# A graph-convolution kernel: every third kept group of the last-but-one pass is sent in pairs, and the sums' rows are asked for earlier

## The chip, the cores and the metric

The kernel runs on one core of a Trainium2 chip. Its time is the device time of one launch in microseconds (us); of several runs the median is taken. Five engines work side by side, each through its own instructions in order, and wait for each other by semaphores: PE (TensorE, matrix products), DVE (VectorE), ACT (ScalarE), POOL (GpSimd, which here issues indirect DMAs) and SP (SyncE, which here issues plain DMAs).

## The reference

It is one message-passing layer on 12,500 nodes and 400,000 edges. The edges are sorted by `dst`, while `src` is random. `h` is gathered by `dst`, and the messages are summed by `src`.

```python
h = relu(layernorm(x))                              # [12500, 128]
h = h @ W_in2f.T
W = smu(edge_attr_20 @ W_f1.T + b_f1) @ W_f2.T + b_f2   # [400000, 128]
msg = h[dst] * W * edge_weight[:, None]
agg = segment_sum(msg, src, 12500)
out = x + smu(agg @ W_o1.T + b_o1) @ W_o2.T + b_o2
# smu(x) = ((1 + a) * x + (1 - a) * x * erf(mu * (1 - a) * x)) / 2,  a = 0.01, mu = 2.5
```

## The kernel before

**Units.** 128 edges are a tile, 4 tiles a group, 2 groups (8 tiles) a super. There are 391 supers (782 groups; the last has one tile). The supers are cut into ten passes of 56, 56, 56, 56, 46, 36, 36, 26, 16 and 7 supers (`PARTS`). The nodes are cut into 98 bins of 128.

**Sending.** A message is a row of 129 floats: 128 values and the place of its node inside its bin, plus a mark of the pass. It is written by an indirect DMA on POOL (`scatter_rows`, L1005; called a scatter from here on) into a buffer in DRAM, to row bin x capacity + slot. One scatter sends one tile, so 128 rows. The slot is a running count: `bins` adds up on DVE how often each bin has come (`so`), `count` turns that into a rank with triangular matrices on PE, `read` and `number` make the row index `ix` on DVE.

**Summing.** When a whole pass has been sent, its rows are read back while the next pass is sent. `begin` and `fetch` (L1036, SP) read the rows of several bins at once into one of four `rw` buffers (774 KB for passes whose sums take 12 rows per partition). `choose` (L1050, DVE) makes the 0/1 matrix `se` of which row belongs to which node. `add` (L1063, PE) multiplies the two per bin into a PSUM bank `pg` of four bins, and DVE adds the bank to `agg` (L1076). A new `fetch` is asked for when a buffer has been used up. `chores` says in which group of a pass these things begin: `times` returns the group at which the rows are asked for, the one at which the first `se` is made, and the one at which the products begin. From there the products are spread evenly over the rest of the pass (`lo`, `hi`, `parts`). The products of pass 7 are 98 bins x 3, those of pass 8 are 98 bins x 2; the trace shows each product as two records. From pass 7's sums on, each finished bank of the older sum is also multiplied by `w_o1` (`fold`, L1089, and a copy on ACT, L1090).

**Paired groups.** In passes 1 to 7 every 4th group (`EVERY`) is paired. Rows of its tiles 0 and 1 are matched with rows of tiles 2 and 3 that go to the same bin, so that two rows stand side by side and one scatter sends 128 pairs. `spread_keys` and `match` find the partners (PE, DVE), `rank_left` and `place_left` number the rows that are left, `permute` (L794, PE) brings the rows into order, and `take_pairs` (L805, L806, ACT) copies them out of PSUM. The rows that are left over make one more tile, `lt`, which is sent with a later group of the same pass (its "host"), where it is also counted. A paired group so takes 3 scatters and not 4.

**Kept groups.** The last two passes (8 and 9, `SENT_LAST`) are computed early: after every ninth super of passes 1 to 4 stands one super of these. Their messages, already multiplied by `w_o1`, are stored as `kept_rows` in DRAM, and their indices stay in `ix_kept`. When all other groups have been sent, the **closing loop** goes through these 46 groups. For each one, `refill` (L1665, SP) reads back the rows of the group four ahead into one of six `ms` buffers, `chores` sets up the sums of the pass before, `scatter` sends the group's four tiles, and `parts` does its share of the products. Before the loop stands a chain of small operations that forms a flag (L1668 to L1685). Behind the loop the last stage sums pass 9 and applies the output layer (L1716 to L1760).

**What sets the order.** Every engine but POOL goes through its instructions in the order in which the code is written; so does each queue. SP's reads for the sums and SP's refills stand in one queue, one behind the other.

```python
        for g in range(g1, NG):
            refill(g + 4)
            k = chores(g)
            scatter(g, back.pop(g))
            parts(hi)
            if g - g1 >= 2:
                old(g - g1 - 2)
            biased(g - g1 - 10)
```

## Time and profile before

| | |
|---|---|
| three runs | 5584.23, 5608.95 and 5618.83 us; median 5608.95 us |
| the profiled execution | 5585.07 us, of which the span from the first to the last instruction is 5583.3 us |
| mean granted TensorE clock | 0.82 of full speed |
| busy in the span | PE 69%, DVE 59%, POOL 53%, ACT 50% |
| scatters | 2668 and 138 before the closing loop, 181 in it |
| closing loop | first scatter at 5207.23 us, last one at 5509.91 us, end of the program at 5583.3 us |

Times in the rows are us from the start of the span, the length of one operation in a group is in ns. "busy, mean | idle before <-releaser" says how long a group of instructions was busy, how long one took, and how long the engine had stood idle just before them, with what ended most of it. Releaser "issue" means that the engine waited for nothing that the profile shows, "remote" that the releaser isn't among the recorded instructions. In the view by stretches, (x) is the number of records that begin or run in a stretch, PEclk the granted TensorE clock, and DMA share the busy part of the 16 DMA engines.

### The profile page before, as it was taken

How to read it: one execution, taken by the hardware profiler on the slowest of the kernel's cores; microseconds unless marked ns; L12 is line 12 of the kernel's file. 1: busy time of each engine (PE TensorE's matmuls, PEld its weight loads, DVE VectorE, ACT ScalarE, POOL GpSimd, SP SyncE). 2: the span in 40 equal slices, each digit the busy share in tenths (PEclk: the TensorE clock that was granted, in tenths of full speed). 3: DMA queues.
4: the chain of work that ended last, by engine and by line, in shares of the span. 5: the costliest groups of instructions: out<-in, count | busy, mean ns of one | idle time of the engine just before them, and what ended most of it. 6: DMA issues, size and time to landing. Idle time of an engine off the chain costs nothing. (4 is left out here: it accounts for less than half of the span.)

```text
span 5583.3 us, 86344 instructions
## 1 busy us (share of the span) xinstructions
PE 3853.0 (69%) x26034; PEld 3229.5 (58%) x26034; DVE 3306.8 (59%) x8547; ACT 2787.6 (50%) x7401; POOL 2934.9 (53%) x3031
## 2 busy tenths in 40 slices
PE   7566667667776776666776677777777667676557
PEld 3245446556665665555665566666666556566446
DVE  7766555556556666555666566656665556565336
ACT  6544455555555555555555555555454545544101
POOL 5556554544545555555545455455455555554564
PEclk9767778888888888888888788888888888888778
DMA  5756655556655555554555455555555545554567
GB/s 145 200 172 186 189 161 168 175 169 182 176 158 150 156 149 162 150 154 144 154 155 159 146 160 160 154 164 154 161 157 156 151 137 154 148 158 143 175 207 204
DMA packets 660449, 907.51 MB, mean 163 GB/s; under 512 B 181219, under 2 KB 446823, under 8 KB 659849
## 3 DMA queue, kind: packets, MB, share of 16 engines
q1 hardware_dynamic: 552553, 673.46, 42.5%
q0 software_dynamic: 100112, 216.17, 11.8%
q10 hardware_dynamic: 7312, 12.29, 0.6%
q8 instruction: 211, 3.46, 0.3%
q14 instruction: 261, 2.14, 0.1%
HBM read 507.13 MB, written 394.46 MB: 161 GB/s over the span
## 5 line engine op out<-in xcount | busy, mean ns | idle before, releaser
L1005 POOL DMA_INDIRECT buf<-ms,ix x2668 | 2587.5, 970 | 1898.6 <-issue 939.5
L880 ACT ACTIVATE hg<-ph,w_sb 128x128 f32<-128x128 f32 x2784 | 794.1, 367 | 1987.8 <-remote 1078.9
L1063 PE MATMUL pg<-se,rw 128*128 128x128 f32 x8232 | 1405.3, 313 | 507.6 <-DVE agg L1076 258.1
L1063 PEld LDWEIGHTS pg<-se,rw 128*128 128x128 f32 x8232 | 1248.3, 221 | 665.9 <-issue 296.2
L905 PE MATMUL pw<-w_f,ge 128*128 128x128 f32 x5568 | 1216.5, 345 | 443.2 <-DVE ms L935 382.9
L905 PEld LDWEIGHTS pw<-w_f,ge 128*128 128x128 f32 x5568 | 1022.4, 229 | 551.9 <-issue 326.5
L652 DVE SCALAR_TENSOR_TENSOR so<-irow_ps,hi_f,so 128x98 f16<-128x98 f32 x2846 | 902.6, 317 | 85.3 <-PE pg L825 3.9
L716 DVE TENSOR_REDUCE sl<-pc 128x4 f32<-128x392 f32 (+1 forms) x782 | 451.7, 578 | 591.5 <-remote 311.8
L935 DVE TENSOR_TENSOR ms<-pw,hg 128x512 f32<-128x512 f32 x558 | 383.1, 687 | 671.2 <-issue 414.9
L1050 DVE TENSOR_TENSOR se<-irow_ps,rw 128x1536 f32<-128x1536 f32 (+1 forms) x353 | 601.8, 1705 | 177.4 <-remote 114.6
L906 PE MATMUL pw<-wls,f 128*128 128x128 bf16 x2784 | 679.7, 244 | 2.6 <-issue 2.6
L601 ACT ACTIVATE oh<-oh,onesb 128x512 bf16<-128x512 bf16 x746 | 538.1, 721 | 24.2
L600 ACT ACTIVATE oh<-rbc,nrow 128x512 bf16<-128x512 uint8 x728 | 542.4, 745 | 0.0
L1005 POOL DMA_INDIRECT buf<-lt,ix x138 | 132.2, 958 | 578.6 <-DVE ix L739 566.3
L861 PE MATMUL ph<-hw,oh 126*128 126x128 bf16 x2784 | 311.4, 241 | 167.0 <-issue 106.7
L861 PEld LDWEIGHTS <-oh 126*128 126x128 bf16 x2784 | 244.3, 110 | 209.9 <-issue 188.2
L1076 DVE TENSOR_TENSOR agg<-agg,pg 128x512 f32<-128x512 f32 (+1 forms) x200 | 134.4, 673 | 384.1 <-remote 277.0
L906 PEld LDWEIGHTS <-f 128*128 128x128 bf16 x2784 | 316.9, 114 | 1.8 <-issue 1.8
L833 ACT ACTIVATE ge<-pu 128x512 f32<-128x512 f32 x448 | 273.2, 610 | 42.9 <-PE pu L825 13.4
L683 PE MATMUL pc<-so,tri 128*128 128x392 f16 (+1 forms) x644 | 234.7, 364 | 29.2 <-issue 19.6
L794 PE MATMUL pt<-cd,mt 128*128 128x129 f32 (+1 forms) x1656 | 233.0, 295 | 23.9 <-DVE at L774 22.3
L1005 POOL DMA_INDIRECT buf<-ms,ix_kept x181 | 174.5, 964 | 133.8 <-DMA ms<-kept_rows 81.6
(317 smaller groups left out, 4450.0 us busy)
## 6 DMA issues: line engine op xcount, KB each, us to landing
rw<-buf SPq DMA_DIRECT2D x300, 774.0 KB
f<-f_parts SPq DMA_DIRECT2D x370, 240.0 KB
buf<-zero SPq DMA_DIRECT2D x146, 387.0 KB
rbc<-rel_dram SPq DMA_DIRECT2D x389, 128.0 KB
buf<-ms,ix POOLq DMA_INDIRECT x2668
f_parts<-hs SPq DMA_DIRECT2D x106, 360.0 KB
rw<-buf SPq DMA_DIRECT2D x49, 645.0 KB
f_parts<-hs SPq DMA_DIRECT2D x108, 240.0 KB
```

The lines of the kernel that those rows point to most:

```text
L600: nc.scalar.activation(oh, loaded[s][1][:, o:o + n], AF.Abs, bias=pneg if s < FEW // SUP else nrow)
L601: nc.scalar.activation(oh, oh, AF.Relu, scale=-1.0, bias=onesb[:, 0:1])
L652: nc.vector.scalar_tensor_tensor(so[:, j], irow_ps[:, :NB], hi_f[:, t + j:t + j + 1], since, op0=ALU.is_equal, op1=ALU.add)
L716: nc.vector.tensor_reduce(sl[:, :n], pc[:, :n], op=ALU.max, axis=AX.X)
L861: nc.tensor.matmul(ph[:, j * P:(j + 1) * P], oh[:3 * WIN, a:a + P], hw[:3 * WIN, g % PER, :], start=True, stop=True)
L880: nc.scalar.activation(hg[:, j * P:(j + 1) * P], rows_of[g][:, j * P:(j + 1) * P], AF.Copy, scale=w_sb[:, t + j:t + j + 1])
L905: nc.tensor.matmul(pw[:, a:a + P], ge[:, a:a + P], w_f2, start=True, stop=False)
L906: nc.tensor.matmul(pw[:, a:a + P], fb[:, o + a:o + a + P], wls, start=False, stop=True)
L935: nc.vector.tensor_tensor(ms[:, :n, 0:P], pw.rearrange("p (j f) -> p j f", f=P)[:, :n], hg.rearrange("p (j f) -> p j f", f=P)[:, :n], op=A ...
L1005: i = nc.gpsimd.indirect_dma_start(out=(wide if g in host or g in paired else bufs)[k][:, :], out_offset=bass.IndirectOffsetOnAxis(ap=ix, ...
L1050: nc.vector.tensor_tensor(se[:, a:a + n], own.unsqueeze(1).to_broadcast([P, n, P]), rows_in[c][:, a:a + n, P:P + 1].to_broadcast([P, n, P] ...
L1063: nc.tensor.matmul(pgs[0][:, g, :], rows_in[c][:, o, 0:P], sel[c][:, o, :], start=(q == 0), stop=(q == Q[k] - 1))
```

## The change

- One super moves from pass 8 to pass 0 (`PARTS`: 57 and 15 for 56 and 16). The closing loop so has 44 groups instead of 46, and the loop before it two more that scatter.
- In pass 8 every third group (`LATE_EVERY`), eight in all, is paired. The matching is done in the closing loop when the group is sent: its keys are kept from before (`late_keys`), `spread_keys` and `match` stand two groups ahead of it, `permute` and `take_pairs` one group ahead. `refill` reads such a group in two halves, `ms` and `cd`.
- The rows that are left over aren't counted with a host. They are counted behind all others of the pass: `count_left` goes on from the pass's last count (`so_end`), `place_of_left` makes the index, and the scatter stands three groups behind the pair's own.
- `times`: the rows of pass 7 are asked for at group 1 of pass 8 instead of 2, and the products begin at group 2 instead of 4; for pass 8 and the groups of pass 9 it is 0 instead of 1, and 0 instead of 4.
- In the closing loop `chores` stands ahead of `refill`, and `parts` is cut in two halves.
- The flag is formed at the last group of pass 8, not before the loop. The old inputs that the last stage needs are kept in other places, since `mt` is in use. A row of ones (`ones1`) gives way to a row of another constant.

The diff, cut to what moves work (`g in paired` became `g in pair_no` in the functions that are left out):

```diff
-PARTS = (56, 56, 56, 56, 46, 36, 36, 26, 16, 7)
+PARTS = (57, 56, 56, 56, 46, 36, 36, 26, 15, 7)
 EVERY = 4
+LATE_EVERY = 3
...
+        LATE_END = eps_of[-1][0] * PER - 1
+        late_pairs = list(range(EARLY * PER + LATE_EVERY - 1, LATE_END - 3, LATE_EVERY))
+        pair_no = {g: i for i, g in enumerate(list(paired) + late_pairs)}
...
-            if g in paired:
+            if g in pair_no:
                 last[k] = so[:, GRP]
                 nc.vector.scalar_tensor_tensor(so[:, GRP], so[:, 1], 2.0, before, op0=ALU.mult, op1=ALU.add)
+            if g == LATE_END:
+                nc.vector.tensor_copy(so_end, last[k])
...
-            if g in paired:
-                key = cnt.tile([P, GRP], F32, name="key")
+            if g in pair_no:
+                key = cnt.tile([P, GRP], F32, name="key") if g in paired else late_keys[:, late_pairs.index(g)]
                 nc.vector.scalar_tensor_tensor(key, sl[:, :n], BIG + CAP[k] - 2, hic[:, t - t0:t - t0 + n],
                                                op0=ALU.min, op1=ALU.add)
                 keys_of[g] = key
+                if g not in paired:
+                    nc.scalar.activation(ix[:, :2], key[:, :2], AF.Copy)
                 return
...
-            return (2, 3, 4) if k == EPOCHS - SENT_LAST else (1, 2, 4)
+            return (1, 1, 2) if k == EPOCHS - SENT_LAST else (0, 0, 0)
...
                 back[g] = msg.tile([P, GRP, ROW], F32, name="ms")
+                if g in pair_no:
+                    t0, hic = begins[epoch[s_of(g)]]
+                    cd = apart_of[g] = msg.tile([P, 2, ROW + 1], F32, name="cd", bufs=2)
+                    nc.sync.dma_start(back[g][:, 0::2, :], kept_rows[:, t - kept_tile:t - kept_tile + 2, :])
+                    nc.sync.dma_start(cd[:, :, 0:ROW], kept_rows[:, t - kept_tile + 2:t - kept_tile + 4, :])
+                    nc.scalar.activation(cd[:, :, P + 1], hic[:, t + 2 - t0:t + 4 - t0], AF.Identity, bias=shift)
+                    mixed[g] = back[g]
+                    return
                 nc.sync.dma_start(back[g][:, :n, :], kept_rows[:, t - kept_tile:t - kept_tile + n, :])
...
+        def count_left(g):
+
+            i = late_pairs.index(g)
+            so = rings[1][:, i % 8]
+            rows_of_bins(epoch[s_of(g)])
+            nc.vector.scalar_tensor_tensor(so, bin_row, left_of[g][1], since[0], op0=ALU.is_equal, op1=ALU.add)
+            pc = of_left[g] = ps1.tile([P, GRP * P], F32, name="pc")[:, :NB]
+            nc.tensor.matmul(pc, tri, so, start=True, stop=False, skip_group_check=True)
+            nc.tensor.matmul(pc, rest_h, since[0], start=False, stop=True, skip_group_check=True)
+            since[0] = so
+
+        def place_of_left(g):
+
+            k = epoch[s_of(g)]
+            sl = cnt.tile([P, GRP + 1], F32, name="sl")
+            nc.vector.tensor_reduce(sl[:, 0:1], of_left.pop(g), op=ALU.max, axis=AX.X)
+            ix = ranks[g] = cnt.tile([P, GRP + 1], I32, name="ix", bufs=8)
+            nc.vector.scalar_tensor_tensor(ix[:, 0:1], sl[:, 0:1], BIG + CAP[k] - 1, left_of[g][1],
+                                           op0=ALU.min, op1=ALU.add)
...
         for g in range(g1, NG):
+            k = chores(g)
             refill(g + 4)
-            k = chores(g)
+            if g + 2 in late_pairs:
+                spread_keys(g + 2)
+                match(g + 2)
+            if g + 1 in late_pairs:
+                permute(g + 1)
+                take_pairs(g + 1)
             scatter(g, back.pop(g))
+            if g - 3 in late_pairs:
+                scatter_rows(g - 3, left_of.pop(g - 3)[0], ranks.pop(g - 3)[:, 0:1])
+            parts(lo + (hi - lo) // 2)
+            if g + 2 in late_pairs:
+                rank_left(g + 2)
+                place_left(g + 2)
+            if g in late_pairs:
+                number_left(g)
+                count_left(g)
             parts(hi)
+            if g - 1 in late_pairs:
+                place_of_left(g - 1)
+            if g == LATE_END:
+                limits_of(epoch[s_of(g)], since[0])
+                nbad = flag_formed()
```

How the change moves instructions, at the three places that the prediction uses.

POOL in the closing loop (`buf_65` is the buffer of pass 8, `buf_63` that of pass 9, `lt` a tile of rows left over; 30974 rows instead of 25088 mark a paired scatter or one of left-over rows). Before:

```order
L1005 DMA buf_64<-lt,ix 43518x129
L1005 DMA buf_64<-ms,ix 43518x129 x4
L1005 DMA buf_64<-ms,ix 37632x129 x24
L1005 DMA buf_65<-ms,ix_kept 25088x129 x128
L1005 DMA buf_63<-ms,ix_kept 12544x129 x53
```

And with the change, from the same place (the first three paired groups of eight):

```order
L1020 DMA buf_64<-ms,ix 37632x129 x24
L1020 DMA buf_65<-ms,ix_kept 25088x129 x16
L1020 DMA buf_65<-ms,ix_kept 30974x129 x2
L1020 DMA buf_65<-ms,ix_kept 25088x129 x8
L1020 DMA buf_65<-lt,ix 30974x129
L1020 DMA buf_65<-ms,ix_kept 30974x129 x2
L1020 DMA buf_65<-ms,ix_kept 25088x129 x8
L1020 DMA buf_65<-ms,ix_kept 30974x129 x2
L1020 DMA buf_65<-lt,ix 30974x129
```

Three groups that took 12 scatters take 11: two for the pair, eight for the two others, one for left-over rows.

SP at the head of the closing loop (`rw<-buf_64` are the reads of pass 7's rows, `ms<-kept_rows` and `cd<-kept_rows` the refills, `f<-in_x` old inputs). Before:

```order
L1036 DMA rw<-buf_63 128x2x516
L1665 DMA ms<-kept_rows 128x516 x7
L1036 DMA rw<-buf_64 128x4x387 x4
L309 DMA f_142<-in_x 128x4x128
L1665 DMA ms<-kept_rows 128x516
```

With the change:

```order
L1051 DMA rw<-buf_63 128x2x516
L1688 DMA ms<-kept_rows 128x516 x2
L1683 DMA ms<-kept_rows 128x2x129
L1684 DMA cd<-kept_rows 128x2x129
L1688 DMA ms<-kept_rows 128x516 x2
L1051 DMA rw<-buf_64 128x4x387 x4
L1683 DMA ms<-kept_rows 128x2x129
L1684 DMA cd<-kept_rows 128x2x129
```

Five groups are refilled ahead of the four reads of pass 7, where seven were.

PE in the closing loop, in the middle of pass 7's sums. Before there are only products and folds:

```order
L1063 MATMUL pg_55646<-se,rw 128x128 x12
L1089 MATMUL pu<-agg,w_o_107 128x512
L1063 MATMUL pg_55674<-se,rw 128x128 x12
L1089 MATMUL ph<-agg,w_o_107 128x512
L1063 MATMUL pg_55702<-se,rw 128x128 x12
```

With the change, from one paired group's `spread_keys` (L763) over `rank_left` (L782, L783) to the `permute` (L809) of the same group and the next products of the sums:

```order
L763 MATMUL pt<-ident,late_keys 128x128 x2
L1078 MATMUL pg_55896<-se,rw 128x128 x5
L782 LDWEIGHTS tri
L782 MATMUL pt<-h_first,tri 128x2
L783 LDWEIGHTS ones_h
L783 MATMUL pt<-h_first,ones_h 128x1
L1078 MATMUL pg_55896<-se,rw 128x128 x6
L1104 MATMUL ph<-agg,w_o_106 128x512
L809 MATMUL pt<-cd,mt 128x129 x4
L809 MATMUL pt<-cd,mt 128x130 x2
L1078 MATMUL pg_55960<-se,rw 128x128 x12
L1104 MATMUL pu<-agg,w_o_106 128x512
```

A pair's products now stand between those of the sums, in their order, and the pair's scatter on POOL stands behind `permute`.

More of the change, by code (lines that the diff above doesn't have):

```diff
@@ L649, in bins @@
                 since = before if j == 0 else so[:, j - 1]
-                if g in paired and j % 2 == 0:
+                if g in pair_no and j % 2 == 0:
                     since = none
@@ L696, in count, with limits_of @@
                 nc.vector.tensor_scalar(bad[:, 3:4], mm[:, 0:1], float(ZMIN[0]), None, op0=ALU.is_gt)
-            if g + 1 in first or g + 1 == NG:
-                k = epoch[g // PER]
+            if (g + 1 in first or g + 1 == NG) and g != LATE_END:
+                limits_of(epoch[g // PER], after)
+        def limits_of(k, after):
                 pt = ps1.tile([P, GRP, P], F32, name="ph")[:, 0, :NB]
@@ L1005, in scatter_rows @@
                 i = nc.gpsimd.indirect_dma_start(
[L1006 removed]
+                    out=(wide if g in host or g in pair_no else bufs)[k][:, :],
                     out_offset=bass.IndirectOffsetOnAxis(ap=ix, axis=0), in_=rows, in_offset=None)
@@ L1679, in gnn_kernel @@
-        nc.vector.tensor_scalar(bad[:, 1:2], ends[:, 1:2], float(WIN - 1), None, op0=ALU.is_gt)
-        bs = const.tile([P, 1], F32, name="bs")
-        nc.vector.tensor_reduce(bs, bad, op=ALU.add, axis=AX.X)
-        pn = ps1.tile([P, GRP * P], F32, name="pc")[:, 0:1]
-        nc.tensor.matmul(pn, onesb, bs, start=True, stop=True)
-        nbad = const.tile([P, 1], I32, name="nbad")
-        nc.vector.tensor_copy(nbad, pn)
+                if g in pair_no:
+                    t0, hic = begins[epoch[s_of(g)]]
[5 more added lines that the diff above has]
+                    return
@@ new lines, in gnn_kernel @@
+        since, of_left, ranks = [so_end], {}, {}
+        def count_left(g):
[7 more added lines that the diff above has]
+            since[0] = so
@@ L1834, in gnn_kernel @@
                 pw = gps.tile([P, P], F32, name="gpw")
-                nc.tensor.matmul(pw, ones1[:, :P], b2row, start=True, stop=False)
+                nc.tensor.matmul(pw, onesb[0:1], b2row, start=True, stop=False)
                 nc.tensor.matmul(pw, sm, w_f2, start=False, stop=True)
```

75 lines of the change are left out of this document (43 added, 32 removed).

## The prediction

> **What bounds the kernel now.** I read the page first, then the timelines of POOL, SP and PE in the closing loop, then the waits and the stretches of that loop. On the page:
>
> ```profile
> span 5583.3 us, 86344 instructions
> L1005 POOL DMA_INDIRECT buf<-ms,ix x2668 | 2587.5, 970 | 1898.6 <-issue 939.5
> L1005 POOL DMA_INDIRECT buf<-ms,ix_kept x181 | 174.5, 964 | 133.8 <-DMA ms<-kept_rows 81.6
> ```
>
> Nearly all the change happens in the closing loop: its 181 scatters are busy for 174.5 us and POOL stands idle for 133.8 us, 81.6 of it for refilled rows. POOL's own timeline there (start, length, wait in front):
>
> ```profile
> 5207.23 0.95 POOL L1005 DMA_INDIRECT buf<-ms,ix_kept  x1 [4.64 <-DMA ms<-kept_rows]
> ...
> 5241.35 0.96 POOL L1005 DMA_INDIRECT buf<-ms,ix_kept  x1 [0.30 <-issue]
> 5255.55 0.96 POOL L1005 DMA_INDIRECT buf<-ms,ix_kept  x1 [13.24 <-DMA ms<-kept_rows]
> ...
> 5284.62 0.96 POOL L1005 DMA_INDIRECT buf<-ms,ix_kept  x1 [0.30 <-issue]
> 5296.34 0.96 POOL L1005 DMA_INDIRECT buf<-ms,ix_kept  x1 [10.76 <-DMA ms<-kept_rows]
> ...
> 5415.47 0.96 POOL L1005 DMA_INDIRECT buf<-ms,ix_kept  x1 [0.30 <-issue]
> 5416.74 0.96 POOL L1005 DMA_INDIRECT buf<-ms,ix_kept  x1 [0.30 <-issue]
> ...
> 5509.91 0.96 POOL L1005 DMA_INDIRECT buf<-ms,ix_kept  x1 [4.77 <-DMA ms<-kept_rows]
> ```
>
> 28 scatters in a row begin from 5207.23 to 5241.35, so one follows the other after 34.12 / 27 = 1.264 us. Then the refilled groups are used up and POOL stands. The next cycle is 24 scatters (six groups, 24 x 1.264 = 30.3 us) and a hole, 5255.55 to 5296.34 = 40.8 us. The 129th scatter, the first of pass 9, begins at 5416.74: the 32 groups of pass 8 take 209.5 us, 6.55 each. Why the refills are late, from the waits from 5195 to 5530 us (us in total, times, longest) and SP's timeline:
>
> ```profile
> POOL buf L1005 <- DMA ms<-kept_rows: 81.6, 11, 13.7
> SPq L1036 <- remote: 138.2, 11, 29.2
> SPq L1036 <- PE pg L1063: 75.9, 23, 21.3
> PE pg L1063 <- issue: 88.5, 62, 24.1
> ```
>
> ```profile
> 5202.73 12.91 SPq L1665 DMA_DIRECT2D ms<-kept_rows  x7
> 5215.66 31.88 SPq L1036 DMA_DIRECT2D rw<-buf  x4
> ...
> 5409.00 10.39 SPq L1665 DMA_DIRECT2D ms<-kept_rows  x5
> 5419.51 32.93 SPq L1036 DMA_DIRECT2D rw<-buf  x4
> ```
>
> A refill stands in SP's queue behind a read of sum rows, and that read waits until PE has used up a buffer (75.9 us; another 138.2 are put down to nothing recorded). So PE sets when SP goes on, and SP when POOL does. What PE does meanwhile:
>
> ```profile
> 5258.10 2.84 PE L1063 MATMUL pg<-se,rw 128*128 128x128 f32 x24
> 5261.64 2.84 PE L1063 MATMUL pg<-se,rw 128*128 128x128 f32 x24
> ...
> 5276.77 0.37 PE L1063 MATMUL pg<-se,rw 128*128 128x128 f32 x1 [0.81 <-issue]
> 5278.18 0.37 PE L1063 MATMUL pg<-se,rw 128*128 128x128 f32 x1 [1.03 <-issue]
> ```
>
> ```profile
> core 0: us, PE busy (x) PEld busy (x) DVE busy (x) ACT busy (x) POOL busy (x), PEclk, DMA share, GB/s
> 5250.00:5268.00 18.00, 15.59 (x102) 13.68 (x101) 8.05 (x7) 1.20 (x2) 9.60 (x10) 0.88 1.02 324
> 5268.00:5290.00 22.00, 7.64 (x24) 6.11 (x24) 0.57 (x1) 0.53 (x1) 13.42 (x14) 0.50 0.33 103
> 5290.00:5310.00 20.00, 19.14 (x115) 15.63 (x116) 13.55 (x14) 2.45 (x5) 10.20 (x11) 0.87 1.01 327
> ```
>
> At full pace a bank of 24 records with its fold takes 5261.64 - 5258.10 = 3.54 us. From about 12 us after POOL begins a run of scatters, PE starts one product every 1.4 us with no visible reason ("issue"), 24 records in 22 us, and it recovers about when POOL stands. So the bound is a loop: POOL's run slows PE, slow PE holds SP's read, the read holds the refill, and POOL runs dry. Of a cycle's 40.8 us POOL's scatters take 30.3 and six groups' banks at full pace 6 x 25/28 x 3.54 = 19.0 (25 banks are spread over 28 groups): the two overlap by only 30.3 + 19.0 - 40.8 = **8.5 us**.
>
> **The change, step by step**, against the profiled execution's 5585.07 us.
>
> *Scatters.* Three groups of pass 8 take 11 and not 12, and the moved super takes 8 scatters out of the loop and into pass 0. POOL per three groups: 11 x 1.264 = 13.9 us.
>
> *What a pair adds on PE.* The same operations earlier in the program:
>
> ```profile
> L748 PE MATMUL pt<-ident,key 128*128 128x128 f32 x276 | 65.5, 326 | 85.2 <-DVE key L732 40.7 <-issue 22.3 <-DVE se L1050 10.2
> L794 PE MATMUL pt<-cd,mt 128*128 128x129 f32 (+1 forms) x1656 | 233.0, 295 | 23.9 <-DVE at L774 22.3 <-ACT hs L1507 0.9 <-issue 0.4
> L757 DVE SCALAR_TENSOR_TENSOR mt<-pt,key,onesb 128x256 f32<-128x256 f32 x276 | 121.9, 478 | 70.3 <-PE pt L748 23.0 <-remote 14.1 <-PE pg L1063 7.7
> L775 DVE TENSOR_TENSOR mt<-irow_ps,at 128x256 f32<-128x256 f32 x138 | 58.6, 424 | 4.7
> ```
>
> Per pair (138 of them) `spread_keys` costs PE 65.5/138 = 0.47 us and `permute` 233.0/138 = 1.69; the ranks and counts are a few small products, so 2.2 us is the least. If PE also stands for both halves of `match` (2 x 0.478), for `place_left` (0.42) and once for DVE's previous `se`, it is up to 5. I take 3.5, nearer the rows of busy time, since a group of products lies between most of these steps. Eight pairs: 28 us of PE time.
>
> *The added wait.* The pair's first scatter waits on POOL for ACT's `take_pairs`, that for `permute`, and `permute` stands in PE's order behind the products of the groups ahead. Behind that scatter stand on POOL the next groups' scatters; for these in turn SP's refills wait (six `ms` buffers), and behind the refills the next read of sum rows. Before, PE could lag five groups; now about two. The order of `chores` ahead of `refill` puts each read ahead of one more refill, in the same direction.
>
> *Sum of pass 8.* If the overlap stays 8.5 us a cycle, and a cycle is now three groups because of that wait: 13.9 + 3 x 25/28 x 3.54 (9.5) + 3.5 - 8.5 = **18.4 us** for three groups, where 19.6 (3 x 6.55) stood. Pass 8 is then 8 x 18.4 + 6 x 6.55 = 186.5 us instead of 209.5: **-23 us**. Ends: no overlap 26.9, POOL's pace 13.9.
>
> *The flow ahead.* Two groups more are sent in pass 0 and one kept super less is computed:
>
> ```profile
> 10.40:738.10 727.70, 62.43 (x113) 0.77 0.62 177
> ...
> 738.10:1537.90 799.80, 72.09 (x125) 0.83 0.58 174
> ```
>
> These are stretches cut at DVE's slot numbers (L716; the length stands behind the stretch, then DVE's busy time for them, clock, DMA share, GB/s): pass 0 with 56 supers, and pass 1 with 56 and six kept ones. A sent super costs 727.7/56 = 13.0 us; six kept ones with the sums beside them cost 72.1, 12.0 each. Between nothing and 8 x 1.264 = 10.1 us: **+4**.
>
> *The boundary to pass 9.* SP's rows show that four reads of 33 us stand behind the refills at both passes' heads. Now they stand ahead of one refill more and only four or five groups lie ready, some 8 scatters less: between 0 and 10 us sooner dry, **+4**.
>
> *The end.* The sums of pass 8 begin at once and not four of 14 groups later. When POOL sends its last row, PE has this left:
>
> ```profile
> 5508.52 20.56 PE L1063 MATMUL pg<-se,rw 128*128 128x128 f32 x176 [0.51 <-DVE se L1050]
> ```
>
> An earlier start can take 0 to 18 of these 20.6 us, if PE isn't behind already, as it mostly is: **-7**.
>
> *At nothing:* the flag, whose product stood ahead of the loop,
>
> ```profile
> 5203.67 0.56 PE L1683 MATMUL pc<-bs,onesb 128*128 128x1 f32 x2 [4.42 <-DVE bs L1681]
> ```
>
> (PE waited 4.42 us there, while POOL waited 4.64 for the first refill in any case) and stands now behind pass 8's last group; the kept pairs' keys, which take DVE's place of the index; the row of ones. Cover is PE's and DVE's idle time beside POOL; without it up to +5.
>
> -23 + 4 + 4 - 7 = **-22**, so 5563 on the profiled execution's scale. That execution is the second fastest of four; their mean (5585.07, 5584.23, 5608.95, 5618.83) is 5599, 14 above it. I put the forecast at 5563 + 14, and a little toward the median shown: **5580 us**.
>
> The section "What's actually happening" of the Trainium skill's page "TensorE: Matmul & The Clock Gate" says that PE falls to half clock after an idle window of some 3.4 us and needs as long a busy one to come back. The stretches agree: 0.50 from 5268 to 5290, 0.87 behind it. It speaks against shorter cycles, which begin twice as often; an estimate from its figure, about 1 us a restart, would make the sum some 8 us worse.
>
> **Rivals.**
>
> *Fast (0.22).* Runs of 11 scatters with a wait between them end after 13.9 us, about when PE's slow time would begin (24 scatters ran before). PE then keeps its pace: 9.5 + 3.5 = 13.0 us fit beside POOL's 13.9, plus half a bank ahead of `permute` (1.8): about 15.5 for three groups, 8 x 15.5 + 39.3 = 163, -46 with the other terms: 5553; with no wait left and all of the end's gain about 5530. Against it: the slow start of products came in every long run, and nothing forces POOL to pause where the pair is ready in time.
> The Trainium skill's page "SBUF — State Buffer", section "Who interferes with whom", holds that PE never waits on another engine for memory, by which PE would always keep pace and this case would be the likeliest. The trace speaks against it: 24 records in 22 us beside 14 scatters.
>
> *PE paces (0.14).* The saved scatters only make the holes longer: pass 7's products need their 209 us in any case, and 4 + 4 - 7 is left: about 5600.
>
> *Slower: lockstep (0.20).* `permute` stands behind the products, the pair's scatter behind `permute`, the next read behind the refills. If PE's slow time moves with it, nothing overlaps: 26.9 us for three groups, 8 x 26.9 + 39.3 = 254.5, +45, with +4 and up to +10 at the boundary and nothing gained at the end +59: 5658. It makes the kernel slower from about 21 us per three groups, and by over 1% from 28. For it: PE is the late one in every cycle. Against it: the matching is asked for two groups ahead.
>
> That the change doesn't do what it says can't be: the order shows one scatter less per three groups.
>
> **How the numbers follow.** Forecast 0.44, rivals as given. Forecast bounds: the pair at 2.2 or 5 (-10, +12), flow and boundary 0 or +10 each, end 0 or -18. The range reaches into the fast case (5530) and into the lockstep (5640). 1%, 56 us, is about what a measurement of this kernel can tell from no change: below 5553 lies two thirds of the fast case and a little of the forecast, 0.18; above 5665 over half of the lockstep's 0.20 with its worse ends, 0.14.
>
> **What would show it.** 157 `ix_kept` scatters and 146 of `lt`; POOL's holes ended by ACT's copies and not by refilled rows alone; three groups in some 18 us; fewer than 176 records of PE behind the last scatter. Right or wrong is decided by the granted clock and the count of records in stretches beside POOL's runs: near 100 in 18 us all along means the fast case, PE's "issue" time above 88.5 us the lockstep. What I can't price is why PE is slow beside long runs; if it hangs on bytes in flight and not on the run's length, every term of pass 8 moves.

## The result, and the profile after

| | before | after |
|---|---|---|
| median of 22 runs each | 5588.23 us (5550.69 to 5618.83) | 5570.14 us (5547.67 to 5618.14) |
| ratio | | **0.9968**, 95% interval 0.9952 to 0.9983 |
| profiled execution, its span | 5585.07, 5583.3 us | 5568.72, 5567.0 us |

The change makes the kernel faster by 0.32%, 18 us (by the interval 10 to 27), so within 1%. The two profiled executions differ by 16.4 us. On the page after, the scatters:

```profile
span 5567.0 us, 86766 instructions
L1020 POOL DMA_INDIRECT buf<-ms,ix x2676 | 2587.0, 967 | 1891.5 <-issue 984.8
L1020 POOL DMA_INDIRECT buf<-lt,ix x146 | 139.6, 956 | 602.8 <-DVE ix L754 584.8
```

and, from the groups by line, those of the closing loop:

```profile
L1020 POOL DMA_INDIRECT buf<-ms,ix_kept x157 | 152.9, 974 | 113.7 <-DMA ms<-kept_rows 57.4 <-issue 46.2 <-ACT lt L821 9.2
```

The counts are as foretold: eight scatters more ahead of the loop, 157 + 8 = 165 instead of 181 in it. POOL's idle time in front of these scatters fell from 133.8 to 113.7 us. Another 13.5 us stand in front of the eight `lt` scatters of the loop, so that POOL as a whole stands only 6.6 us less (127.2 us), and most of what it gains in the loop is the sixteen scatters that aren't sent. Refilled rows still end most of the waits (57.4 us instead of 81.6); the added wait for ACT's copies of a pair's left-over rows ends 9.2 us. POOL's timeline after (start, length, wait in front):

```profile
5212.36 0.95 POOL L1020 DMA_INDIRECT buf<-ms,ix_kept  x1 [6.87 <-DMA ms<-kept_rows]
...
5235.98 0.96 POOL L1020 DMA_INDIRECT buf<-ms,ix_kept  x1 [3.72 <-ACT lt L821]
...
5244.59 0.96 POOL L1020 DMA_INDIRECT buf<-ms,ix_kept  x1 [6.39 <-DMA ms<-kept_rows]
...
5285.94 0.96 POOL L1020 DMA_INDIRECT buf<-ms,ix_kept  x1 [7.62 <-DMA ms<-kept_rows]
...
5308.79 0.96 POOL L1020 DMA_INDIRECT buf<-ms,ix_kept  x1 [0.30 <-issue]
5316.76 0.96 POOL L1020 DMA_INDIRECT buf<-lt,ix  x1 [7.00 <-issue]
...
5405.78 0.96 POOL L1020 DMA_INDIRECT buf<-ms,ix_kept  x1 [0.30 <-issue]
...
5492.23 0.96 POOL L1020 DMA_INDIRECT buf<-ms,ix_kept  x1 [0.30 <-issue]
```

The holes are shorter (2 to 11 us instead of 2 to 14) and there are more of them (14 of over 1.2 us instead of 9). The row at 5405.78 is the 113th of the loop, the first scatter of pass 9; both kernels send 53 there. With the rows of before this gives the stages:

| us | before | after | difference | forecast |
|---|---|---|---|---|
| flow, up to the first `ix_kept` scatter | 5207.2 | 5212.4 | +5.1 | +4 |
| pass 8, up to the first scatter of pass 9 | 209.5 | 193.4 | -16.1 | -23 |
| pass 9, up to the end of the last scatter | 94.1 | 87.4 | -6.7 | +4 |
| last stage, up to the end of the span | 72.4 | 73.8 | +1.4 | -7 |

The sum, -16.3 where -22 was forecast, is better than its parts: pass 9 went the other way than forecast, and the last stage gained nothing. What PE does beside a run of scatters, in stretches (as before: PE, PEld, DVE, ACT, POOL busy with counts, clock, DMA share, GB/s):

```profile
5285.90:5297.90 12.00, 8.86 (x61) 8.21 (x60) 5.79 (x8) 1.88 (x5) 9.21 (x10) 0.82 0.99 292
5297.90:5309.90 12.00, 3.23 (x13) 2.21 (x12) 0.00 (x0) 0.00 (x0) 9.11 (x10) 0.64 0.26 92
5309.90:5321.90 12.00, 9.19 (x42) 8.21 (x42) 6.20 (x13) 1.71 (x5) 2.87 (x3) 0.55 0.48 135
```

POOL's run here is 19 scatters long, 5285.94 to 5309.75. In its first 12 us PE has 61 records (a product of the sums is two), in the next 12 only 13, and in the 12 behind its end 42. The slow time of PE is still there; the pairs have only cut the runs. Nor is it a matter of the sums alone. The matching on DVE, and the products around it on PE:

```profile
5294.35 0.69 DVE L315 TENSOR_TENSOR f<-f,bo 128x512 f32<-128x512 f32 x1
5309.94 0.48 DVE L772 SCALAR_TENSOR_TENSOR mt<-pt,late_keys,onesb 128x256 f32<-128x256 f32 x1 [14.90 <-remote]
```

```profile
5297.30 0.63 PE L763 MATMUL pt<-ident,late_keys 128*128 128x128 f32 x2
...
5300.52 0.61 PE L1078 MATMUL pg<-se,rw 128*128 128x128 f32 x4
5310.89 0.16 PE L782 MATMUL pt<-h_first,tri 128*128 128x2 f16 x1 [9.76 <-DVE mt L772]
```

DVE's `match` needs `spread_keys` (L763), whose record on PE ends at 5297.93. It begins at 5309.94, 0.19 us after POOL's last scatter of the run. The profile names no recorded releaser for this wait ("remote"). I read it so that PE's result came to DVE 12 us late, beside the run; the next step of the pair, `rank_left` on PE (L782), then waited for `match` (9.76 us).

### The profile page after: what moved, and what is told of

It reads as the page before. It is cut to its first block, busy times and chain, and to the rows that moved or that the text cites. A ratio compares the mean times of both kernels' runs of the same rounds, so it can differ in the third digit from the quotient of the medians.

```text
span 5567.0 us, 86766 instructions
## 1 busy us (share of the span) xinstructions
PE 3873.5 (70%) x26189; PEld 3255.9 (58%) x26189; DVE 3324.1 (60%) x8641; ACT 2790.8 (50%) x7433; POOL 2920.1 (52%) x3023
## 5 line engine op out<-in xcount | busy, mean ns | idle before, releaser
L1020 POOL DMA_INDIRECT buf<-ms,ix x2676 | 2587.0, 967 | 1891.5 <-issue 984.8
L607 ACT ACTIVATE oh<-oh,onesb 128x512 bf16<-128x512 bf16 (+1 forms) x745 | 537.4, 721 | 24.2
L809 PE MATMUL pt<-cd,mt 128*128 128x129 f32 (+1 forms) x1752 | 254.0, 300 | 37.9 <-DVE at L789 30.6
L809 PEld LDWEIGHTS pt<-cd,mt 128*128 128x128 f32 x1752 | 238.1, 215 | 48.2 <-issue 28.1
```

Of the source, the lines that this page charges most:

```text
L607: nc.scalar.activation(oh, oh, AF.Relu, scale=-1.0, bias=onesb[:, 0:1])
L809: nc.tensor.matmul(po[:, j * (ROW + 1):j * (ROW + 1) + w], pp[:, o:o + P], cd[:, i, :w], start=(i == 0), stop=(i == 1))
L1020: i = nc.gpsimd.indirect_dma_start(out=(wide if g in host or g in pair_no else bufs)[k][:, :], out_offset=bass.IndirectOffsetOnAxis(ap=ix, ...
```

## The experiments

Each profile gives the same four stages, from its POOL timeline: the first `ix_kept` scatter, the 53rd last one, the end of the last one, the end of the span.

| kernel | scatters in pass 8 | flow | pass 8 | pass 9 | last stage | loop and last stage | ratio to before (95%) |
|---|---|---|---|---|---|---|---|
| before | 128 | 5207.2 | 209.5 | 94.1 | 72.4 | 376.1 | |
| after | 112 | 5212.4 | 193.4 | 87.4 | 73.8 | 354.6 | 0.9968 (0.9952 to 0.9983) |
| one super moved | 120 | 5227.5 | 206.1 | 81.8 | 74.3 | 362.2 | 0.9991 (0.9969 to 1.0013) |
| times only | 128 | 5214.2 | 209.1 | 100.0 | 74.0 | 383.1 | 0.9995 (0.9976 to 1.0014) |
| all but the pairs | 120 | 5207.6 | 191.1 | 99.4 | 68.5 | 359.0 | 0.9986 (0.9963 to 1.0009) |
| pairs only | 119 | 5210.9 | 201.5 | 97.8 | 84.2 | 383.5 | 1.0005 (0.9989 to 1.0021) |
| memsets (sent as before) | 128 | 5202.5 | 212.3 | 93.8 | 77.9 | 384.0 | 0.9984 (0.9966 to 1.0002) |
| narrow rows | 128 | 5224.7 | 208.6 | 94.7 | 75.2 | 378.5 | |
| refills by ACT | 128 | 5224.8 | 225.9 | 67.3 | 102.1 | 395.3 | 1.0017 (0.9994 to 1.0040) |
| after, stops in pass 9 | 112 | 5292.5 | 194.0 | 97.8 | 69.6 | 361.4 | 0.9943 (0.9923 to 0.9963) |

Each row is one execution. Each ratio is to the kernel before on the same chip; the four kernels from "one super moved" to "pairs only" ran on one chip, the next three on a second, the last on a third, while the kernel before has one profile only. The memset kernel sends pass 8 as the kernel before does (below), and its loop and last stage take 384.0 us against 376.1. So a difference of some 8 us in that sum can be that of two executions, and one of 22 us in the flow (5202.5 and 5224.7 with the same `PARTS`).

**One super moved.**

```diff
-PARTS = (56, 56, 56, 56, 46, 36, 36, 26, 16, 7)
+PARTS = (57, 56, 56, 56, 46, 36, 36, 26, 15, 7)
```

> The kernel before with one super moved from pass 8 to pass 0, nothing else. By the forecast's terms pass 8 loses two groups at 6.55 us (-13.1 us: from 209.5 to about 196 us) and the flow ahead gains 4 to 5 us, so the time falls by about 8 us (ratio 0.9985). If PE paces (pass 7's products need their 209 us whatever the number of groups), pass 8 stays near 209 us and the kernel is 4 to 5 us slower (ratio 1.001).

The time falls by 5 us (interval -17 to +7), in the expected direction but not clear of nothing. Pass 8 gives 3.4 us and not 13.1, which is nearer to the case that PE paces. But the line between passes 8 and 9 shifts from kernel to kernel, since POOL can run dry on either side of it; the two passes together take 287.9 us where they took 303.6, 15.7 less. Loop and last stage together give 14 (22 against the memset kernel).

**The times alone.**

```diff
-            return (2, 3, 4) if k == EPOCHS - SENT_LAST else (1, 2, 4)
+            return (1, 1, 2) if k == EPOCHS - SENT_LAST else (0, 0, 0)
```

> The kernel before with the two rows of times alone, (1, 1, 2) and (0, 0, 0). The prediction had +4 us at the head of pass 9 and -7 us at the end, -3 us together. The trace with the whole change has pass 9 6.7 us shorter and the end 1.4 us longer: if that comes from the times, pass 9 falls from 94 to about 87 us here and the time by about 5 us (ratio 0.999). If it comes from the pairs' lead or the order of the chores, this kernel stays as before (1.000).

Pass 9 becomes longer here, 100.0 us, and not shorter: by this one profile the four reads ahead of the refills cost 5.9 us, near the +4 of the prediction, and nothing comes back at the end (74.0). The 6.7 us that the change's own trace gains in pass 9 aren't the times'.

**All but the pairs.**

```diff
-        late_pairs = list(range(EARLY * PER + LATE_EVERY - 1, LATE_END - 3, LATE_EVERY))
+        late_pairs = []
...
-        late_keys = const.tile([P, len(late_pairs), GRP], F32, name="late_keys")
+        late_keys = const.tile([P, 1, GRP], F32, name="late_keys")
```

> The changed kernel with an empty list of late pairs: the super moved, the times, the order of the chores and the flag as in the change, but pass 8 sends all its groups with four scatters. By the forecast the pairing saves 19.6 - 18.4 = 1.2 us for three groups, 10 us in all, so this kernel is 10 us slower than the changed one (ratio to the kernel before about 0.9985). If PE paces, the pairing is worth nothing: ratio as the changed kernel, 0.997. If the pairs cost their PE time (3.5 us each), it is faster than the changed kernel by up to 28 us (ratio 0.992).

Loop and last stage take 359.0 us without the pairs and 354.6 with them, 4 us less. By the ratios (0.9986 and 0.9968) the pairing is worth the 10 us of the forecast, but the two intervals leave room from some 25 us for it to 5 against it. So the size agrees, and a gain isn't shown.

Nor does it lie where the prediction had it. Pass 8 takes 191.1 us without the pairs and 193.4 with them, though eight scatters fewer are sent; pass 9 is 12.0 us shorter with them, the last stage 5.3 longer. What the pairs change in pass 8 is PE's work. Here are the stretches of pass 8 and the waits from 5195 to 5515 us, first without the pairs, then with them:

```profile
5207.63:5398.73 191.10, 114.55 (x650) 93.91 (x649) 67.48 (x66) 11.95 (x20) 116.57 (x121) 0.74 0.69 218
PE pg L1078 <- issue: 94.6, 58, 21.6
PE pg L1078 <- DVE agg L1091: 13.3, 4, 5.0
```

```profile
5212.36:5405.78 193.42, 137.23 (x851) 118.56 (x851) 89.78 (x150) 19.29 (x45) 109.34 (x112) 0.80 0.72 220
PE pg L1078 <- issue: 15.8, 8, 7.0
PE pg L1078 <- DVE agg L1091: 40.1, 7, 13.5
```

PE stands for 76.6 us of pass 8 without the pairs and for 56.2 with them, and its waits for nothing that the profile shows nearly vanish, while those for DVE's addition grow. So with its runs cut by the pairs POOL holds PE up less. PE has 201 records more in pass 8 and 146 more up to the end of the program (1641 and 1495), which are the pairs' own; the other 55 are work of the sums that is done earlier. A second profile with pairs (the kernel with stops in pass 9) has 65.8 us of PE idle time there. From the loop's first scatter to the end PE is busy for 228.3 us without the pairs and for 240.3 with them, 1.5 us for each of eight.

**The pairs alone.** The changed kernel with the old `PARTS` and the old `times`.

```diff
-PARTS = (57, 56, 56, 56, 46, 36, 36, 26, 15, 7)
+PARTS = (56, 56, 56, 56, 46, 36, 36, 26, 16, 7)
...
-            return (1, 1, 2) if k == EPOCHS - SENT_LAST else (0, 0, 0)
+            return (2, 3, 4) if k == EPOCHS - SENT_LAST else (1, 2, 4)
```

> The changed kernel with the old PARTS and the old times: the pairs, their order and the flag's new place remain. By the forecast it is about 10 us faster than the kernel before (ratio 0.998), with three groups in 18.4 us. If PE paces, no difference (1.000, three groups in 19.6 us). If the pairs cost their PE time, up to 28 us slower (1.005, 23 us).

The forecast's 0.998 lies outside the interval (0.9989 to 1.0021). With 16 supers there are nine pairs and 119 scatters, and pass 8 takes 201.5 us, 8.0 less than before; the last stage takes 11.8 us more. But this kernel also has more to sum. The room that a bin gets for a pass's rows (`CAP`: the rows to be expected and a margin) is rounded up to a multiple of 128 rows. With 15 supers, or with 16 and no pairs, it comes to 256 rows for pass 8, with 16 supers and pairs to 384. So pass 8's sums need 98 x 3 products here and not 98 x 2. The page of the change has the first of these rows, that of the pairs alone the second:

```profile
L1078 PE MATMUL pg<-se,rw 128*128 128x128 f32 x8232 | 1418.2, 315 | 454.4 <-DVE agg L1091 217.9
L1078 PE MATMUL pg<-se,rw 128*128 128x128 f32 x8428 | 1427.4, 313 | 451.0 <-DVE agg L1091 250.7
```

These are 196 records more. At the pace of the row that the kernel before has behind its last scatter (176 records in 20.56 us) they take some 23 us of PE. PE's end shows them, here first the rows of the kernel with pairs only, then those of all but the pairs, then those of the change:

```profile
5507.79 4.96 PE L1078 MATMUL pg<-se,rw 128*128 128x128 f32 x43
5513.84 26.51 PE L1078 MATMUL pg<-se,rw 128*128 128x128 f32 x228 [1.09 <-issue]
```

```profile
5502.48 9.38 PE L1078 MATMUL pg<-se,rw 128*128 128x128 f32 x80 [0.51 <-DVE se L1065]
```

```profile
5496.28 16.34 PE L1078 MATMUL pg<-se,rw 128*128 128x128 f32 x120 [6.21 <-DVE agg L1091]
```

Behind POOL's last scatter (it ends at 5510.25, 5498.14 and 5493.19) PE needs 30 us in the first, 14 in the second, 19 in the change, 18 in the kernel before. The 12 us more of the first are less than its added products cost. So its ratio holds for the pairs together with a third product for every bin of pass 8, and what the pairs alone are worth it doesn't show.

**No scatters in pass 8.** In the loop the scatters of pass 8 are left out.

```diff
-            scatter(g, back.pop(g))
+            if epoch[s_of(g)] == EPOCHS - SENT_LAST:
+                taken.pop(g)
+                back.pop(g)
+            else:
+                scatter(g, back.pop(g))
```

> The kernel before without the 128 scatters of pass 8 in the closing loop (left out, so pass 8's rows are missing in the sums); refills, reads and products stay. It shows PE's own pace in pass 7's sums. If POOL's runs slow PE, PE's issue waits vanish between the head of the loop and pass 9, the granted clock is above 0.85 and the 32 groups need about 28 x 25/28 x 3.54 = 89 us plus the four reads at the head (33 us, mostly waiting), some 100 to 125 us instead of 209.5. If PE is slow for a reason of its own (its code, the reads' data), the products still need some 180 us or more.

One execution takes 5486.91 us where the kernel before has 5600.31 on the same chip. POOL stands from its last row of pass 7, at 5213.16, to the first of pass 9:

```profile
5213.16 0.96 POOL L1005 DMA_INDIRECT buf<-ms,ix  x1 [0.31 <-issue]
5321.86 1.40 POOL L1005 DMA_INDIRECT buf<-ms,ix_kept  x1 [107.74 <-issue]
```

The stretch behind the head of the loop, and PE's waits from 5195 to 5322 us:

```profile
5246.00:5322.00 76.00, 74.27 (x536) 61.72 (x535) 60.13 (x62) 12.50 (x21) 0.14 (x1) 1.00 1.08 357
PE pg L1063 <- issue: 2.2, 1, 2.2
```

Pass 7's sums need 108 us and not 209 when POOL sends nothing, with PE busy for 74 of the last 76 us at a clock of 1.00 and with 2.2 us of issue waits where the kernel before has 88.5 (5195 to 5530 us). So it is the scatters that slow PE. 128 of them fill 128 x 1.264 = 162 us; with them pass 8 takes 102 us more, so that only 60 of the 162 are hidden beside PE's work.

**Narrow rows.** The scatters of pass 8 send 43 of a row's 129 values.

```diff
+NARROW = 43
...
+                to = (wide if g in host or g in paired else bufs)[k][:, :]
+                if k == EPOCHS - SENT_LAST:
+                    to, rows = to.rearrange("a (t r) -> (a t) r", r=NARROW), rows[:, 0:NARROW]
...
-                    out=(wide if g in host or g in paired else bufs)[k][:, :],
+                    out=to,
```

> The kernel before, in which the scatters of pass 8 send the first 43 of a row's 129 values to places three times as dense (so pass 8's rows are missing in the sums): as many rows and as long on POOL, a third of the bytes. If PE is slow beside long runs because of the bytes in flight, the slow stretches go (PE's issue wait of 88.5 us in the loop falls below 30, pass 8 takes 165 us, 40 less). If it hangs on POOL's run of descriptors or on their number, the slow stretches stay where they are, from 8 to 12 us after a run's begin, and pass 8 takes 200 to 210 us.

Pass 8 takes 208.6 us, and PE's issue wait is 96.3 us from 5200 to 5530. So by this one execution the bytes of a scatter aren't what slows PE.

**A short pause.** A memset on POOL behind every second group of pass 8.

```diff
+        still = edge.tile([P, GRP * P], F32, name="ge")
...
+            if epoch[s_of(g)] == EPOCHS - SENT_LAST and (g - g1) % 2 == 1:
+                for _ in range(1):
+                    nc.gpsimd.memset(still, 0.0)
```

> The kernel before with one 128x512 memset on POOL (about 1 us) after every second group of pass 8, so that no run of scatters is longer than eight (10 us). If the length of a run without a pause decides and a pause of some 1 to 2 us is enough, PE is no longer slowed: two groups take 8 x 1.264 + 1.3 = 11.4 us, pass 8 16 x 11.4 = 183 us, ratio about 0.995. If PE needs POOL to stand for some 4 us, PE is slowed as before and pass 8 stays at about 205 to 212 us, ratio 1.000.

The edit didn't do what it was meant to. POOL's instructions don't stand in written order, and since nothing tied the memsets (0.53 us each) to the scatters, all 16 stand ahead of pass 8; the runs are as long as before (28, 24, 24). It serves as a second profile of the kernel before.

**Refills by ACT.**

```diff
-                nc.sync.dma_start(back[g][:, :n, :], kept_rows[:, t - kept_tile:t - kept_tile + n, :])
+                nc.scalar.dma_start(back[g][:, :n, :], kept_rows[:, t - kept_tile:t - kept_tile + n, :])
```

> The kernel before with the refills issued by ACT, not by SP, so that they no longer stand behind the reads of sum rows. By the chain that the prediction read (PE holds the read, the read holds the refill, POOL runs dry) POOL's waits for refilled rows (81.6 us) mostly go, its run gets long, and PE then is slow throughout: pass 8 and 9 send their 181 scatters in 230 to 260 us instead of 303.6, but what PE has left behind the last scatter grows from 176 records by as much as it was slowed, so that the gain at the end is small (0.997 to 1.000). If POOL isn't held by SP's order, POOL's waits stay above 60 us and nothing changes.

The first run of scatters is now 52 long (eight of pass 7 and 44 of pass 8) and the last one 53, and PE all but stands still beside both:

```profile
5226.00:5262.00 36.00, 4.09 (x17) 3.83 (x18) 3.91 (x11) 0.00 (x0) 27.45 (x29) 0.50 0.42 119
```

```profile
5517.76 3.79 PE L1063 MATMUL pg<-se,rw 128*128 128x128 f32 x16 [36.81 <-issue]
```

17 records in 36 us, and at the end a wait of 36.81 us that ends with POOL's last scatter (5518.0). POOL's waits for refills fall only to 61.5 us, and the 181 scatters take 293 us where 230 to 260 were expected. For the refills now stand in ACT's order, and ACT waits for PE as well:

```profile
5305.19 0.60 ACT L1090 ACTIVATE agg<-pu 128x512 f32<-128x512 f32 x1 [90.70 <-PE pu L1089]
```

So the edit moved the refills from one place behind PE to another. Pass 8 is 16 us longer, pass 9 27 us shorter, and the last stage 30 us longer. Nothing is gained: what POOL won in pass 9 by running on, PE owed behind it.

**Stops that hold the scatters up, long and short.** One copy on POOL (three in the long one) of a tile that the group's scatters then read.

```diff
+            if epoch[s_of(g)] == EPOCHS - SENT_LAST and (g - g1) % 2 == 0:
+                for _ in range(1):
+                    nc.gpsimd.tensor_copy(back[g], back[g])
             scatter(g, back.pop(g))
```

> The kernel before, in which POOL copies one refilled tile onto itself (128x516, about 1.2 us) ahead of every second group of pass 8, and the group's scatters wait for it: no run of scatters is longer than eight. If the length of a run decides and 1.5 us are enough to end it, PE keeps its pace: two groups take 10.1 + 1.5 = 11.6 us, pass 8 about 186 us, ratio 0.995 or better. If such a short stop resets nothing, PE is as slow as before, pass 8 takes 205 to 215 us and the ratio is 1.000 to 1.003.

> As the short stop, with three copies (about 4 us) ahead of every second group of pass 8. PE recovered about 4 us after a run's end in the traces; if the run's length decides, PE's issue waits in pass 8 fall from some 80 us below 20, two groups take 10.1 + 4 = 14.1 us and pass 8 about 226 us, with PE never late. If what counts is scatters per time and not the run, PE's issue waits stay above 50 us.

**Two supers moved.** The changed kernel with `PARTS` 58 and 14.

> The changed kernel with two supers moved from pass 8 to pass 0 instead of one (58 and 14). One super moved alone shortened the loop with the end from some 380 us (376.0 in the kernel before, 384 and 379 in two kernels that sent pass 8 alike) to 362, and the flow grew by some 5. If the gain is the work that left the loop, a second super gives about as much again: loop and end at 340 to 345 us where the changed kernel has 354.6, ratio to the kernel before about 0.995. If the first move only filled a gap (PE then paces pass 7's products in fewer groups), loop and end stay at 350 to 355 and the kernel is 5 us slower than the changed one, ratio 0.998.

These three ran on another chip, on which the *kernel before* takes 3933.28 us (median of 20 runs, 3925.53 to 3939.73), not 5590. The short stops give 1.0024 (1.0013 to 1.0035), the long ones 3965.97 us in one execution, two supers moved 0.9983 (0.9973 to 0.9993). Nothing here can test whether a stop frees PE, since PE isn't slowed there. Pass 8 and pass 9 with two supers moved:

```profile
3660.11 0.96 POOL L1020 DMA_INDIRECT buf<-ms,ix_kept  x1 [0.31 <-issue]
...
3792.63 0.95 POOL L1020 DMA_INDIRECT buf<-ms,ix_kept  x1 [0.30 <-issue]
```

```profile
3660.00:3792.00 132.00, 106.23 (x766) 91.95 (x766) 86.08 (x154) 19.25 (x43) 100.47 (x104) 0.93 0.98 310
```

POOL sends without a hole, 104 scatters in 132.5 us, 1.274 each, and PE has 766 records in the same time. The loop goes at POOL's pace, so that a scatter saved there should be worth 1.27 us. The changed kernel itself didn't run on this chip, so what the second super is worth, on this or on the other chips, stays open. The flow ends at 3660.1 us, where the two kernels with stops, which have the old `PARTS`, end it at 3642.8 and 3644.0: a super moved forward costs 8.0 to 8.7 us.

**Stops in pass 9 of the changed kernel.**

```diff
+            if epoch[s_of(g)] == EPOCHS - 1 and (g - g1) % 2 == 0:
+                nc.gpsimd.tensor_copy(back[g][:, :groups[g][1]], back[g][:, :groups[g][1]])
             scatter(g, back.pop(g))
```

> The changed kernel with one copy on POOL (about 0.9 us, as with the short stops of pass 8) ahead of every second group of pass 9, so that no run of scatters there is longer than eight; pass 8 is as in the change. On a chip where a run of POOL slows PE (kernel before near 5590 us): if a short stop ends the slow time, pass 9 takes some 53 x 1.264 + 7 x 0.9 = 73 us where the changed kernel has 87.4, and PE starts 20 or more products per 4 us within it; if not, pass 9 stays at 85 to 95 us with stretches of under 5 products per 4 us. On a chip where PE isn't slowed (kernel before near 3933 us): pass 8 goes at POOL's pace with the change too, 112 x 1.264 = 142 us, three groups in 13.9 us, where the kernel before would need 128 x 1.264 = 162 us; against it the flow has one super more (about 9 us), and the ratio is 0.998 with the stops' 6 us in it.

This chip is again one of the slow kind (the kernel before at 5680.89 us). A copy takes 0.6 us and makes a hole of 0.9. It ends nothing, here behind the stops at 5496.36 and at 5547.58 (the row in the middle is the ten us ahead of the second):

```profile
5496.40:5507.10 10.70, 0.00 (x0) 0.00 (x0) 0.00 (x0) 0.00 (x0) 8.28 (x9) 0.50 0.15 50
5537.00:5547.00 10.00, 6.16 (x40) 5.77 (x38) 3.29 (x5) 0.00 (x0) 7.59 (x9) 0.83 0.75 231
5548.00:5558.00 10.00, 2.48 (x12) 1.99 (x10) 1.05 (x2) 0.00 (x0) 7.59 (x9) 0.53 0.51 158
```

Behind the stop at 5496.36 PE has no record for 10.7 us, while POOL sends its next eight. The profile puts this down to DVE's addition, and DVE's own wait to nothing recorded; DVE there adds a bank that PE fills, so I read it as PE's late result again. Behind the other stop 12 records follow on 40. Pass 9 takes 97.8 us, past the 85 to 95 that were expected if a stop ends nothing. Pass 8, which is the change's, takes 194.0 us, as in the change's own profile (193.4). The whole ratio, 0.9943, is not explained by these stages (loop and last stage 361.4 us, more than the change's 354.6); the change itself wasn't run on that chip, so whether the stops or the chip make it lower stays open.

## Why the prediction was right, and where only its sum was

**The total.** Forecast was -22 us from the profiled execution; -16.4 between the profiles and -18 (-27 to -10) between the medians came. 5580 us stands against 5570.14. That it came so near is in part luck, since the terms missed to both sides: pass 8 gained 7 us less than forecast and the last stage 8 less, while pass 9 came out 11 better.

**The bound** was read rightly as far as it was tried. Leaving out the scatters took 102 us out of pass 8, and with refills that no longer stand behind the reads POOL's runs grew to 52 and 53 scatters and PE all but stood, with no gain. The "about 12 us after POOL begins a run" is 10 to 15 us in three runs of the kernel before (begun at 5207.23, 5255.55 and 5296.34 us, with few records of PE from about 5222, 5265 and 5310).

**Pass 8, -23.** The direction is right, and so is the allowance of some overlap that stays. The 16 scatters that are no longer sent take 20.2 us, and pass 8 became 16.1 shorter. The three groups came to (193.4 - 39.3) / 8 = 19.3 us instead of 18.4, with the same allowance for the six other groups. The division isn't borne out: "three groups 18.4 where 19.6 stood" puts the pairing's 10 us into pass 8, and pass 8 is no shorter with the pairs (193.4) than without them (191.1). Passes 8 and 9 together tell more: 303.6 us before (306.1 in the memset kernel), 287.9 with the super alone, 290.5 with all but the pairs, 280.8 with the change. The pairs' part of that is 9.7 us, of which 5.3 come back in the last stage, and it goes with PE's shorter idle time (76.6 to 56.2 us in pass 8), where the sum had a fixed overlap. The 3.5 us of PE time for a pair are 1.5 by PE's busy time, which holds no waits; that is below even the least of 2.2. The rival "PE paces" is right in that fewer scatters alone didn't shorten pass 8, but not in the whole.

**What is whose.** By the profiles the super gives the larger part of the gain (loop and last stage 14 to 22 us less, of which the flow takes back 5 to 9). By the medians only the whole change is clear of nothing; the super alone is -5 us, the times alone -3, all but the pairs -8, each with an interval that holds zero. The order of `chores` and `refill`, the halves of `parts` and the flag's new place were never run alone.

**The flow, +4**, was +5.1 by two profiles that scatter by more than that, and 8.0 to 8.7 us on the quick chip, inside the bounds of 0 and 10 but above the value taken.

**The boundary, +4.** With the times alone pass 9 is 5.9 us longer, without the pairs 5.3, near the term. In the change's own profile it is 6.7 us shorter all the same, which by the stretches above fits what PE no longer owes from pass 8. The kernel with stops has 97.8 there, some 4 of it the stops' (seven holes of 0.9 us where 0.3 stood), so that one execution may differ from the next by as much.

**The end, -7**, didn't come: +1.4 in the change, +1.6 with the times alone. The sign that was named for it did come, 120 records of PE behind the last scatter instead of 176. But PE waited 6.21 us for DVE ahead of them, and they took 16.34 us, so that PE was done 19 us behind POOL where it had been 18.

**The rivals.** *Lockstep* is refuted: three groups took 19.3 us and not 26.9, PE's issue waits fell to 15.8 us and didn't rise above 88.5, and POOL waited 9.2 us in all for the pairs' copies. *Fast* is refuted on the chips of the forecast as it stood: within a run of 19 PE is slow as before from the 12th us on (13 records in 12 us), though the shorter runs do help PE, as it said. On the quick chip it is what happens, though with two supers moved and not with the change itself. The Trainium skill's rule ("SBUF — State Buffer", "Who interferes with whom") that PE never waits on another engine for memory would have let PE keep pace. It didn't on three chips (on one of them 17 records in 36 us beside 29 scatters) and did on the fourth (766 in 132 us beside 104); whether memory is what PE waits for, no run here shows. The restarts of the clock gate ("TensorE: Matmul & The Clock Gate", "What's actually happening"), which by the prediction's estimate would have cost 8 us, can't be seen apart from this.

**What stays open:** what in a scatter slows PE. It isn't the bytes (narrow rows), and a hole of 0.9 us doesn't end it. Fewer rows in a scatter were not tried, and a longer stop only on the chip that doesn't need it.

## What to carry to other kernels

A transfer saved on one engine is a gain only if the work that pays for it is finished, too: price an edit up to the end of the program, not up to the engine's last instruction, and look at what the other engine still owes there. Where two engines hinder each other, the line between two stages shifts from one kernel to the next; compare the stages together. When parts of a change are taken back to see what they are worth, look at what else is worked out from them: the old `PARTS` beside the pairs gave each bin half as much room again, and with it 196 records that neither kernel has. And where an engine loses time to "issue" alone, leave out the suspected neighbour once: that one run (108 us against 209) told more than all the rows.

## What the runs showed of the hardware that was not expected

PE all but stops beside long runs of indirect DMAs from POOL on three of the four chips of the experiments, from some 10 to 15 us after the run begins until about when it ends; then its products go on, and so do the engines that wait for its results. On one chip it doesn't: there POOL sent the 104 scatters of pass 8 without a hole beside 766 records of PE, 23 per 4 us, the granted clock over the program was 0.95 and not 0.82, and the kernel before took 3933 us where it takes 5584, 5600 and 5681 on the other three. The same program is 1.42 times as fast there. The flow ahead of the loop, too, ends at 3643 us (in the kernel with short stops) and not at 5207. Within a run POOL's scatters are as far apart on both (1.27 us); in the flow they follow each other nearly without a hole on the quick chip (865.5 us of idle time in front of 2684, with two supers moved) and not on the other (1891.5 us in front of 2676, in the change). That the flow's difference has the same cause was not tried. A few tenths of a per cent found on one kind of chip needn't hold on the other.
